# Bounding attention scores by channel maxima, in place of a pass for each row's greatest score

## The chip, the cores and the metric

One core of one Trainium2 chip. The metric is the device time of one execution in microseconds (us). The runs of one kernel on one chip agree within some 0.3%. All runs quoted here are fast: none was more than 1.5% above the fastest of its kernel. In the views of the profile PE is TensorE, PEld its loads of weights, DVE VectorE, ACT ScalarE, POOL GpSimd and SP SyncE; a q after the name means the engine's queue. The granted clock is TensorE's, 1.00 being full speed. PSUM is the memory that TensorE writes its results to.

## The reference

Four residual layers on `x` of shape (2, 128, 64, 64) in float32. Two of them hold softmax attention over all 4096 positions; the other two (depthwise convolutions, and quaternion products of Fourier transforms) are not touched by the change.

```python
# layer 0: four heads of 32 channels; q1 and k1 are divided by their norms over the tokens
attn1 = softmax(einsum('bhnc,bhmc->bhnm', q1, k1) * temperature, axis=-1)
out1  = einsum('bhnm,bhmc->bhnc', attn1, v)
# ... a second, small attention over channels, projections, norms
# layer 3: eight heads of 16 channels
a = softmax(einsum('bhcq,bhck->bhqk', q, k) / sqrt(128), axis=-1)
o = einsum('bhqk,bhck->bhcq', a, v)
```

A softmax subtracts something from each row's scores so that the exponentials don't overflow. Any shift gives the same result in exact arithmetic. The kernel before subtracts each row's greatest score; it has to compute all scores once to find that, and a second time to use them.

## The kernel before

Heads lie in groups of partitions, and a block `qm` holds one head's rows of q, zero elsewhere, so that a matmul over all 128 partitions gives one head's scores. The pass for the greatest scores (comments and some arguments cut):

```python
def _max_pass(...):                                   # line numbers in the profile
    for qt in range(NQT):                             # 32 tiles of 128 queries
        qm = blocks[qt % len(blocks)]
        _own_rows(nc, qm, q, ...)                     # GpSimd copies          L163
        for kc in range(NCH):                         # 8 chunks of 512 keys
            for p in range(0, nh, 2):                 # pairs of heads
                ps = ps_pool.tile([128, 2, CH], F32, tag="sp", name="ps_max")
                for jj in range(2):
                    nc.tensor.matmul(ps[:, jj, :], qm[:, p + jj, :],
                                     k[:, kc * CH : (kc + 1) * CH], ...)     # L175
                nc.vector.tensor_reduce(pm[:, p : p + 2, qt, kc], ps, AX.X, ALU.max)  # L182
                yield
    # [cut] for each head: reduce over chunks, negate, transpose, DMA into row d of q
```

The attention then works on the scores with keys in partitions; row `d` of q, times a row of ones in k, subtracts the maximum:

```python
def _attn_pass(...):
    for qb in range(NCH):                             # 8 blocks of 512 queries
        qm = blocks[qb % len(blocks)]
        _own_rows(nc, qm, q, ..., d + 1, nh)
        for kt in range(NQT):                         # 32 tiles of 128 keys
            for p in range(0, nh, 2):
                ps = ps_pool.tile([128, 2, CH], F32, tag="sp", name="ps_s")
                # [cut] two matmuls k-tile x qm                               # L224
                w = p_pool.tile([128, 2, CH], F32, tag="weights", name="weights")
                nc.scalar.activation(w, ps, AF.Exp)                           # L232
                # [cut] two matmuls values x w of the step before, into ps_acc # L207
                yield
```

`top` is the pass for the maxima and `attend` the attention; `_weave(main, side, n)` issues a step of `side` after every n steps of `main`. In layer 0 that is `_weave(top(0), channels_and_values(), 4)`, the pass with the convolutions, then `_weave(attend(0), top(1), 1)` and `attend(1)` alone, for each of two samples; in layer 3 one `top` alone, three woven stages, one `attend` alone.

Of the kernel before, what the change touches and what calls it, by code (L numbers as in the profile page):

```python
# [17 lines left out]
S = H * W  # L18
CH = 512  # tokens of a chunk: one PSUM bank, eight rows of the image
# [5 lines left out]
FROWS = 4  # rows of frequencies of a weight chunk  # L25
# [4 lines left out]
def _blocks():  # L30
    """Constant matrices, by name, each with up to 128 rows."""
    f8 = np.float64
    k = {}
    k["ident"] = np.eye(128)
    k["group"] = np.kron(np.eye(32), np.full((4, 4), 0.25))
    k["center"] = np.eye(128) - 1.0 / 128
    k["mean"] = np.full((128, 128), 1.0 / 128)
    first = dict(k)

    k = {}  # L40
    # Forward over h: rows (w parity, h), columns (w parity, re/im, fh).
    ang = 2 * np.pi * np.outer(np.arange(H), np.arange(FH)) / H
    k["fwd_h"] = np.kron(np.eye(2), np.concatenate([np.cos(ang), -np.sin(ang)], 1))
    # Columns (r, p, i): the channel (r xor p, i) with the sign that W_p has in output r.
    sign = np.array([[1, -1, -1, -1], [1, 1, 1, -1], [1, -1, 1, 1], [1, 1, -1, 1]], f8)
    perm = np.zeros((128, 4, 4, 32))
    for r in range(4):
        for p in range(4):
            for i in range(32):
                perm[(r ^ p) * 32 + i, r, p, i] = sign[r, p]  # L50
    k["perm"] = perm.reshape(128, 512)
    # Forward over w: rows (re/im, w), columns (-im, re, im; fw); of fh and of its mirror image.
    ang = 2 * np.pi * np.outer(np.arange(W), np.arange(FW)) / W
    c, s = np.cos(ang), np.sin(ang)
    k["fwd_w"] = np.concatenate(
        [np.concatenate([s, c, -s], 1), np.concatenate([-c, s, c], 1)], 0
    )
    k["fwd_w_mirror"] = np.concatenate(
        [np.concatenate([s, c, -s], 1), np.concatenate([c, -s, -c], 1)], 0
    )  # L60
    # Back over w: rows (fw, re/im), columns (re/im, w).
    alpha = np.full((FW, 1), 2.0)
    alpha[0] = alpha[-1] = 1.0
    c, s = alpha * c.T, alpha * s.T
    inv = np.stack([np.concatenate([c, s], 1), np.concatenate([-s, c], 1)], 1).reshape(2 * FW, 2 * W)
    k["inv_w"] = inv
    k["inv_w_mirror"] = inv * np.repeat([1.0, -1.0], W)
    # Back over h: rows (re/im, fh).
    ang = 2 * np.pi * np.outer(np.arange(FH), np.arange(H)) / H
    k["inv_h"] = np.concatenate([np.cos(ang), -np.sin(ang)], 0) / (H * W)  # L70
    second = dict(k)

    k = {}
    sel = np.zeros((2, 128, 64))
    for j in range(4):
        for i in range(16):
            sel[j % 2, 32 * j + i, 16 * j + i] = 1
            sel[1 - j % 2, 32 * j + 16 + i, 16 * j + i] = 1
    k["sel_out"], k["sel_sum"] = sel[0], sel[1]
    third = dict(k)  # L80
    return first, second, third


def _packed(blocks):
    """One array of 128 rows, and where each block lies in it."""
    where, at, parts = {}, 0, []
    for name, a in blocks.items():
        full = np.zeros((128, a.shape[1]), np.float32)
        full[: a.shape[0]] = a
        parts.append(full)  # L90
        where[name] = (a.shape[0], at, at + a.shape[1])
        at += a.shape[1]
    return np.ascontiguousarray(np.concatenate(parts, 1)), where
# [12 lines left out]
def _col(nc, pool, src, name):  # L106
    """A vector of 128, one element in each partition."""
    t = pool.tile([128, 1], F32, tag=name, name=name)
    nc.sync.dma_start(t, src.rearrange("(c o) -> c o", o=1))
    return t  # L110


def _weave(main, side, every):
    """Runs `main` with a step of `side` after every `every` steps, then the rest of `side`."""
    for n, _ in enumerate(main):
        if n % every == every - 1:
            next(side, None)
    for _ in side:
        pass


def _group_stats(nc, pool, psum_tile, x, cst, eps_t):
    """Mean and 1 / sqrt(var + eps) of a sample's groups of four channels, per channel."""
# [27 lines left out]
# The heads of a tile lie hs partitions apart. A head has d rows of q and k; row d is 1 in k and  # L151
# minus the row's greatest score in q, and k is zero in what is left. All rows are contracted, q
# being zero in the other heads' rows of a block that one head uses.
# [42 lines left out]
def _attn_pass(nc, p_pool, ps_pool, acc_pool, blocks, q, k, values, hs, d, nh, done):  # L196
    """values(kt, j): what multiplies the weights of head j in key tile kt, with ones for the
    sums. done(qb, acc) takes the products of a block of queries."""
# [18 lines left out]
    for qb in range(NCH):  # L217
        qm = blocks[qb % len(blocks)]
        _own_rows(nc, qm, q, slice(qb * CH, (qb + 1) * CH), hs, d + 1, nh)
# [23 lines left out]
@with_exitstack  # L243
def _layer0(ctx, tc, X, a, cst, eps5):
# [27 lines left out]
    # 1x1 and depthwise 3x3 as one 3x3 convolution: [ci, tap, co].  # L272
# [18 lines left out]
    max_blocks = _zero_blocks(nc, one, 3, NH, 128, "max_block")  # L291

    def inverse_std(pool, y):
        """1 / sqrt(var over channels + eps), in every channel."""
# [25 lines left out]
    def top(t):  # L320
        return _max_pass(nc, small, spp, ident, max_blocks, qs[t], ks[t], HS, D, NH)
# [9 lines left out]
    for b in range(B):  # L331
        x = X[:, b, :]
        with tc.tile_pool(name="l0_xn", bufs=1) as xp, tc.tile_pool(name="l0_ch", bufs=5) as cp:
# [19 lines left out]
            # q1 and k1; the norms over tokens and the temperature go into q1.  # L353
# [17 lines left out]
            for h in range(4):  # L371
# [5 lines left out]
                )  # L377

            def channels_and_values():
                # k2^T q2, summed over the tokens; then its softmax over k2's channels.  # L380
# [52 lines left out]
                # v, the second attention's output, and v with tokens in partitions.  # L433
# [20 lines left out]
            _weave(top(0), channels_and_values(), 4)  # L454

        with tc.tile_pool(name="l0_p", bufs=3) as pp, tc.tile_pool(name="l0_fin", bufs=5) as cp:
            q_blocks = _zero_blocks(nc, cp, 2, NH, CH, "q_block")

            def attend(t):
                # v and ones of an even head, ones and v of an odd one.  # L460
# [3 lines left out]
                def done(qb, ac):  # L464
# [17 lines left out]
                    nc, pp, spp, accp, q_blocks, qs[t], ks[t], values, HS, D, NH, done  # L482
                )

            _weave(attend(0), top(1), 1)
# [18 lines left out]
@with_exitstack  # L504
def _layer1(ctx, tc, X, a, cst, eps5):
# [20 lines left out]
    # t12 has -t10 and +t7.  # L526
# [6 lines left out]
    for b in range(B):  # L533
# [12 lines left out]
        # Pairs of columns with (w parity, h) in partitions; shifts by two columns are whole tiles.  # L546
# [34 lines left out]
        # [a, shift, b], the shifts in falling order.  # L581
# [22 lines left out]
        # The dilated 5x5 straight onto the residual.  # L604
# [29 lines left out]
@with_exitstack  # L634
def _layer2(ctx, tc, X, a, cst, src, eps5):
# [11 lines left out]
    # Transforms over h for fh to 32, the others being conjugates: [channel, b, fh, re/im, w].  # L647
# [32 lines left out]
    # Back over w, rows of frequencies and their mirror images summed: [channel, b, w, re/im, fh].  # L680
    z = one.tile([128, B, W, 2, FH], F32, name="z")
    names = "wxyz"
    for f0 in range(0, H, FROWS):
# [15 lines left out]
        for pair in range(0, FROWS, 2):  # L699
            # (-im, re, im) of what W_p multiplies in output r: [(p, i), row, fw, r, b, 3].  # L700
# [41 lines left out]
        # [(row, o), (r, b), fw, re/im], then with (fw, re/im) in partitions.  # L742
# [37 lines left out]
    # Back over h, onto the residual.  # L780
# [22 lines left out]
@with_exitstack  # L803
def _layer3(ctx, tc, X, a, cst, src, out, eps5):
# [28 lines left out]
    max_blocks = _zero_blocks(nc, one, 3, NH, 128, "max_block")  # L833
# [40 lines left out]
    def attend(b, t, q, k, vt):  # L874
        rows = slice(64 * t, 64 * t + 64)

        # v and ones of an even head, ones and v of an odd one.
# [4 lines left out]
        def done(qb, ac):  # L882
# [14 lines left out]
            nc, pp, spp, accp, q_blocks, q, k, values, HS, D, NH, done  # L897
        )

    def top(q, k):  # L900
        return _max_pass(nc, two, spp, ident, max_blocks, q, k, HS, D, NH)
# [19 lines left out]
def kernel(ctx, tc, a, out, layers=(0, 1, 2, 3)):  # L921
# [3 lines left out]
    for b in range(B):  # L925
        for i in range(4):
            cols = slice(i * (S // 4), (i + 1) * (S // 4))
            nc.sync.dma_start(X[:, b, cols], a["x"][b, :, cols])
# [3 lines left out]
    if 0 in layers:  # L932
        _layer0(tc, X, a, cst, eps5)
    if 1 in layers:
        _layer1(tc, X, a, cst, eps5)
    if 2 in layers:
        _layer2(tc, X, a, cst, a["consts1"], eps5)
    if 3 in layers:
        _layer3(tc, X, a, cst, a["consts2"], out, eps5)
    else:  # L940
        for b in range(B):
            nc.sync.dma_start(out[b], X[:, b, :])
# [3 lines left out]
def _laid_out(inputs):  # L946
    """The inputs in the orders that the chip reads them in."""
# [16 lines left out]
    # Heads of 16 in slots of 32, four a tile, and a one for the greatest scores behind those of k.  # L964
# [8 lines left out]
    # Pairs of heads with ones between them, for the sums.  # L973
# [26 lines left out]
```

## Time and profile before

| | before |
|---|---|
| median of 4 runs | 16,934.2 us (16,918.7 to 16,954.7) |
| busy: TensorE / VectorE / ScalarE | 97% / 29% / 21% of the span |
| matmuls for maxima / scores / values | 6144 each, two instructions apiece |
| mean granted TensorE clock | 0.971 |

The profile is of one execution, with a span of 16,969.8 us. A group's busy time is the union of its instructions; matmuls overlap at their ends, so the pace is better read from how many steps fit into a long stretch. The prediction below shows the lines.

### The profile page before, as it was taken

The numbers are of one execution on the slowest core, as the hardware profiler recorded it, in microseconds if no ns is written. First come the engines' busy times: TensorE is split into PE (matmuls) and PEld (weight loads), VectorE is DVE, ScalarE is ACT, GpSimd is POOL, SyncE is SP. The second block draws the span as 40 slices with busy tenths as digits, with TensorE's granted clock in tenths as the row PEclk, the third lists the DMA queues.
The fourth block names the chain that finished last, engine by engine and source line by source line (L and its number), as shares of the span: only waits on it lengthen the run. The fifth ranks groups of instructions, "written<-read, shape, count | busy, mean of one in ns | idle before, by whom it ended". The sixth has DMA issues, their size and how long they took to land.

```text
span 16969.8 us, 116126 instructions
## 1 busy us (share of the span) xinstructions
PE 16401.0 (97%) x50778; PEld 6151.0 (36%) x50778; DVE 4966.5 (29%) x4328; ACT 3536.5 (21%) x3820; POOL 468.1 (3%) x1029
## 2 busy tenths in 40 slices
PE   8999998999999788899999999999999999999999
PEld 3433322443332246644333333333333333333222
DVE  4432201352320352267422222322223222221000
ACT  1022232102223201100122222222222222222333
POOL 0000000000000100000000000000000000000000
PEclk9999998999999887889999999999999999999999
DMA  0000000000000015400000000000000000000000
GB/s 19 0 0 0 0 0 0 0 0 0 0 1 0 2 17 83 68 2 0 1 1 1 1 1 1 1 1 1 1 1 1 1 1 1 1 1 1 1 1 1
DMA packets 142859, 90.89 MB, mean 5 GB/s; under 512 B 4752, under 2 KB 137616, under 8 KB 142352
## 3 DMA queue, kind: packets, MB, share of 16 engines
q1 hardware_dynamic: 141056, 80.52, 2.9%
q8 instruction: 399, 6.54, 0.2%
q10 hardware_dynamic: 1296, 2.95, 0.1%
q14 instruction: 108, 0.88, 0.0%
HBM read 78.87 MB, written 4.19 MB: 5 GB/s over the span
## 4 chain that ended last, share of the span: by engine, by line
PE 63%; ACT 1%; issue 1%; DVE 0%; POOL 0%; ACTq 0%; DMA 0%; DVEq 0%; POOLq 0%; SPq 0%
PE ps_max L175 22%; PE ps_s L224 21%; PE ps_acc L207 12%; PE ps_freq L735 2%; PE ps_bank L718 1%; PE ps_bank L707 1%; PE ps_bank L614 1%; PE ps_t L585 1%; ACT yt L715 0%; PE ps_bank L622 0%; PE ps_bank L795 0%; PE ps_bank L764 0%; PE ps_bank L572 0%; PE ps_bank L668 0%; PE ps_sp L887 0%
## 5 line engine op out<-in xcount | busy, mean ns | idle before, releaser
L182 DVE TENSOR_REDUCE max_part<-ps_max 128x2 f32<-128x1024 f32 x3072 | 3765.1, 1226 | 7590.7 <-PE ps_max L175 7589.5
L224 PE MATMUL ps_s<-q_block,k 128*128 128x512 f32 x12288 | 5888.7, 602 | 18.6 <-POOL q_block L163 18.6
L175 PE MATMUL ps_max<-k,max_block 128*128 128x512 f32 x12288 | 5842.6, 610 | 11.2 <-ACT weights L232 5.9
L232 ACT ACTIVATE weights<-ps_s 128x1024 f32<-128x1024 f32 x3072 | 3144.9, 1024 | 10551.5 <-PE ps_s L224 10551.4
L175 PEld LDWEIGHTS ps_max<-k,max_block 128*128 128x128 f32 x12288 | 2164.5, 189 | 3662.1 <-issue 2459.3
L224 PEld LDWEIGHTS ps_s<-q_block,k 128*128 128x128 f32 x12288 | 2253.2, 190 | 3313.2 <-issue 2870.5
L207 PE MATMUL ps_acc<-weights,vt 128*32 128x512 f32 (+1 forms) x12288 | 3258.9, 609 | 1.7 <-ACT weights L232 1.7
L207 PEld LDWEIGHTS ps_acc<-weights,vt 128*32 128x32 f32 (+1 forms) x12288 | 497.5, 116 | 2331.9 <-issue 2310.4
L311 PE MATMUL ps_acc<-xn,wc 128*128 128x512 f32 x1440 | 631.3, 594 | 0.0
L470 DVE RECIPROCAL rec<-rec 64x512 f32<-64x512 f32 x32 | 107.0, 3345 | 1468.2 <-ACT rec L469 1468.2
L163 POOL COPY max_block<-q 16x128 f32<-16x128 f32 (+1 forms) x768 | 233.4, 304 | 9288.2 <-PE ps_max L175 8846.6
L885 DVE COPY u<-ps_acc 128x512 f32<-128x512 f32 x32 | 22.1, 690 | 1482.8 <-PE ps_acc L207 1482.8
L311 PEld LDWEIGHTS ps_acc<-xn,wc 128*128 128x128 f32 x1440 | 272.4, 190 | 342.1 <-issue 342.1
L718 PE MATMUL ps_bank<-consts,yt 128*128 128x99 f32 x1024 | 185.5, 338 | 86.2 <-ACT yt L715 86.2
L735 PEld LDWEIGHTS ps_freq<-e,w_r 128*32 128x32 f32 x4224 | 255.8, 153 | 19.0 <-issue 12.7
L735 PE MATMUL ps_freq<-e,w_r 128*32 128x16 f32 x4224 | 259.9, 212 | 2.2 <-DVE e L725 2.2
L735 PE MATMUL ps_freq<-e,w_i 128*32 128x16 f32 x4224 | 255.4, 212 | 0.0
L735 PEld LDWEIGHTS ps_freq<-e,w_i 128*32 128x32 f32 x4224 | 253.0, 157 | 2.8 <-issue 1.4
L163 POOL COPY q_block<-q 17x512 f32<-17x512 f32 (+1 forms) x192 | 115.8, 609 | 4833.5 <-PE ps_s L224 3802.4
L718 PEld LDWEIGHTS ps_bank<-consts,yt 128*128 128x128 f32 x1024 | 160.6, 239 | 219.1 <-ACT yt L715 218.9
L607 DVE SCALAR_TENSOR_TENSOR X<-g,w,X 128x4096 f32<-128x4096 f32 x50 | 234.7, 4693 | 1.8
L725 DVE COPY e<-ps_bank 128x396 f32<-128x396 f32 x128 | 143.4, 1120 | 307.6 <-PE ps_bank L718 307.6
(176 smaller groups left out, 3012.2 us busy)
## 6 DMA issues: line engine op xcount, KB each, us to landing
w_r<-in_L_conv_kr_w SPq DMA_DIRECT2D x16, 528.0 KB, 12.3
w_r<-in_L_conv_kr_x SPq DMA_DIRECT2D x16, 528.0 KB, 11.8
w_r<-in_L_conv_kr_y SPq DMA_DIRECT2D x16, 528.0 KB, 11.9
w_r<-in_L_conv_kr_z SPq DMA_DIRECT2D x16, 528.0 KB, 11.9
w_i<-in_L_conv_ki_w SPq DMA_DIRECT2D x16, 528.0 KB, 5.4
w_i<-in_L_conv_ki_x SPq DMA_DIRECT2D x16, 528.0 KB, 7.7
w_i<-in_L_conv_ki_y SPq DMA_DIRECT2D x16, 528.0 KB, 10.0
w_i<-in_L_conv_ki_z SPq DMA_DIRECT2D x16, 528.0 KB, 11.9
```

The source lines that it names most:

```text
L163: nc.gpsimd.tensor_copy(block[hs * j : hs * j + rows, j, :], q[hs * j : hs * j + rows, cols])
L175: nc.tensor.matmul(ps[:, jj, :], qm[:, p + jj, :], k[:, kc * CH : (kc + 1) * CH], start=True, stop=True,)
L182: nc.vector.tensor_reduce(pm[:, p : p + 2, qt, kc], ps, AX.X, ALU.max)
L207: nc.tensor.matmul(acc[0][r : r + hs, :], values(kt, p + jj), w[:, jj, :], start=(kt == 0), stop=(kt == NQT - 1),)
L224: nc.tensor.matmul(ps[:, jj, :], k[:, kt * 128 : (kt + 1) * 128], qm[:, p + jj, :], start=True, stop=True,)
L232: nc.scalar.activation(w, ps, AF.Exp)
L311: nc.tensor.matmul(out, wc[:, t, grp * C : (grp + 1) * C], xn[:, c * ROWS + t // 3 : (c + 1) * ROWS + t // 3, t % 3 : t % 3 + W], start=(t ...
L585: nc.tensor.matmul(t3[:, lo // 4, : (hi - lo) * C], xt[:, 3 + u, :], xt[:, u + lo : u + hi, :].rearrange("p k c -> p (k c)"), start=(u == ...
L607: nc.vector.scalar_tensor_tensor(xi, g[:, i : i + H, j : j + W], w8[:, s : s + 1], xi, ALU.mult, ALU.add)
L614: nc.tensor.matmul(pv, t9[:, k, :], t2[:, c * ROWS + k : (c + 1) * ROWS + k, 2 : W + 2], start=(k == 0), stop=False,)
L718: nc.tensor.matmul(pe[:, r * 3 * FW : (r + 1) * 3 * FW], yt[:, r * 128 : (r + 1) * 128], k["fwd_w" if fh == m else "fwd_w_mirror"], start= ...
L735: nc.tensor.matmul(out.rearrange("p (x c) -> p x c", c=2), ws[n][:, :, gq * FW + fw], ef[:, :, 1 - n : 3 - n], start=(n == 0), stop=(n == 1),)
```

## The change

A score is a sum over the head's channels of q times k, so it is at most the sum over channels of max|q| times max|k|, maxima over the tokens. That needs two reductions over 4096 elements and one tiny matmul per tile of heads. If all bounds are at most 60, the exponentials can be taken without a shift. If not, a branch at the end runs the full old program, which is compiled in a second time. The core of the diff (two places are put in words; cut are the zeroing of q in layer 0, and that row `d` of q, which held the maximum, is left out of the scores when there is no pass):

```diff
+LIMIT = 60.0
+class _Bounds:
+    def add(self, q, k, heads, psum_tile, small):
+        m = small.tile([128, 2], F32, tag="bd_m", name="bd_m")
+        for i, t in enumerate((q, k)):
+            nc.vector.tensor_reduce(m[:, i : i + 1], t, AX.X, ALU.max, apply_absolute_value=True)
+        p = small.tile([128, 1], F32, tag="bd_p", name="bd_p")
+        nc.vector.tensor_mul(p, m[:, 0:1], m[:, 1:2])
+        ps = psum_tile()
+        nc.tensor.matmul(ps[:, 0:1], heads, p, start=True, stop=True)
+        nc.vector.tensor_copy(self.all[:, self.at : self.at + 1], ps[:, 0:1])
+        self.at += 1
+    def within(self, psum_tile, small, ident):
+        # compare with LIMIT, minimum over columns, transpose, minimum, to int32
 ...
+            if bounds is not None:
+                for t in range(2):
+                    bounds.add(qs[t], ks[t], same_head, acc, small)
-            _weave(top(0), channels_and_values(), 4)
+            if bounds is None: _weave(top(0), channels_and_values(), 4)
+            else: run channels_and_values() alone
-            _weave(attend(0), top(1), 1)
+            _weave(attend(0), top(1) if bounds is None else iter(()), 1)
 ...  # layer 3: top(q, k) becomes bounds.add(q, k, ...) and an empty iterator
+    bounds = _Bounds(nc, keep, 8)
+    layers(bounds)
+    with tc.tile_pool(name="bd_ps", bufs=1, space=PSUM) as ps:
+        flag = bounds.within(...)
+    within = nc.values_load(flag[0:1, 0:1], min_val=0, max_val=1)
+    with tc.If(within < 1):
+        layers(None)
```

More of the change, by code (lines that the diff above doesn't have):

```diff
@@ L147, in _normalized, with _same_head, __init__ @@
     nc.vector.tensor_scalar(out, x, mean, rstd, ALU.subtract, ALU.mult)
+LIMIT = 60.0
+def _same_head(nc, pool, hs):
+    t = pool.tile([128, 128], F32, name="same_head")
+    nc.gpsimd.memset(t, 0.0)
+    for r in range(0, 128, hs):
+        nc.gpsimd.memset(t[r : r + hs, r : r + hs], 1.0)
+    return t
+class _Bounds:
+    def __init__(self, nc, pool, n):
+        self.nc, self.pool, self.at = nc, pool, 0
+        self.all = pool.tile([128, n], F32, name="bounds")
+    def add(self, q, k, heads, psum_tile, small):
+        nc = self.nc
+        m = small.tile([128, 2], F32, tag="bd_m", name="bd_m")
+        for i, t in enumerate((q, k)):
+            nc.vector.tensor_reduce(
+                m[:, i : i + 1], t, AX.X, ALU.max, apply_absolute_value=True
+            )
+        p = small.tile([128, 1], F32, tag="bd_p", name="bd_p")
[5 more added lines that the diff above has]
+    def within(self, psum_tile, small, ident):
+        nc = self.nc
+        assert self.at == self.all.shape[1]
+        ok = small.tile([128, self.at], F32, name="bd_ok")
+        nc.vector.tensor_scalar(ok, self.all, LIMIT, None, ALU.is_le)
+        low = small.tile([128, 1], F32, name="bd_low")
+        nc.vector.tensor_reduce(low, ok, AX.X, ALU.min)
+        ps = psum_tile()
+        nc.tensor.transpose(ps[0:1, 0:128], low, ident)
+        one = small.tile([1, 1], F32, name="bd_one")
+        nc.vector.tensor_reduce(one, ps[0:1, 0:128], AX.X, ALU.min)
+        flag = small.tile([1, 1], mybir.dt.int32, name="bd_flag")
+        nc.vector.tensor_copy(flag, one)
+        return flag
 def _zero_blocks(nc, pool, n, nh, cols, name):
@@ L193, in _max_pass, with _attn_pass @@
     yield
-def _attn_pass(nc, p_pool, ps_pool, acc_pool, blocks, q, k, values, hs, d, nh, done):
+def _attn_pass(nc, p_pool, ps_pool, acc_pool, blocks, q, k, values, hs, rows, nh, done):
     waiting = []
@@ L218, in _attn_pass @@
         qm = blocks[qb % len(blocks)]
-        _own_rows(nc, qm, q, slice(qb * CH, (qb + 1) * CH), hs, d + 1, nh)
+        _own_rows(nc, qm, q, slice(qb * CH, (qb + 1) * CH), hs, rows, nh)
         for kt in range(NQT):
@@ L243, in _layer0 @@
 @with_exitstack
-def _layer0(ctx, tc, X, a, cst, eps5):
+def _layer0(ctx, tc, X, a, cst, eps5, bounds=None):
     nc = tc.nc
@@ L290, in _layer0 @@
             nc.gpsimd.memset(ks[t][HS * j + D : HS * j + D + 1, :], 1.0)
-    max_blocks = _zero_blocks(nc, one, 3, NH, 128, "max_block")
+    if bounds is None:
+        max_blocks = _zero_blocks(nc, one, 3, NH, 128, "max_block")
+    else:
+        for t in range(2):
+            nc.gpsimd.memset(qs[t], 0.0)
+        same_head = _same_head(nc, one, HS)
     def inverse_std(pool, y):
@@ L377, in _layer0 @@
                 )
+            if bounds is not None:
+                for t in range(2):
+                    bounds.add(qs[t], ks[t], same_head, acc, small)
             def channels_and_values():
@@ L452, in channels_and_values @@
                     yield
-            _weave(top(0), channels_and_values(), 4)
+            if bounds is None:
+                _weave(top(0), channels_and_values(), 4)
+            else:
+                for _ in channels_and_values():
+                    pass
         with tc.tile_pool(name="l0_p", bufs=3) as pp, tc.tile_pool(name="l0_fin", bufs=5) as cp:
             q_blocks = _zero_blocks(nc, cp, 2, NH, CH, "q_block")
+            rows_of_q = D + (bounds is None)
             def attend(t):
@@ L481, in attend @@
                 return _attn_pass(
-                    nc, pp, spp, accp, q_blocks, qs[t], ks[t], values, HS, D, NH, done
+                    nc, pp, spp, accp, q_blocks, qs[t], ks[t], values, HS, rows_of_q, NH, done
                 )
-            _weave(attend(0), top(1), 1)
+            _weave(attend(0), top(1) if bounds is None else iter(()), 1)
             for _ in attend(1):
@@ L803, in _layer3 @@
 @with_exitstack
-def _layer3(ctx, tc, X, a, cst, src, out, eps5):
+def _layer3(ctx, tc, X, a, cst, src, out, eps5, bounds=None):
     nc = tc.nc
@@ L831, in _layer3 @@
     nc.sync.dma_start(bv, a["L3_conv_bv"].to_broadcast([128, 192]))
-    max_blocks = _zero_blocks(nc, one, 3, NH, 128, "max_block")
+    if bounds is None:
+        max_blocks = _zero_blocks(nc, one, 3, NH, 128, "max_block")
+    else:
+        same_head = _same_head(nc, one, HS)
     q_blocks = _zero_blocks(nc, one, 2, NH, CH, "q_block")
@@ L896, in attend @@
         return _attn_pass(
-            nc, pp, spp, accp, q_blocks, q, k, values, HS, D, NH, done
+            nc, pp, spp, accp, q_blocks, q, k, values, HS, D + (bounds is None), NH, done
         )
     def top(q, k):
+        if bounds is not None:
+            bounds.add(q, k, same_head, lambda: sp()[:, 0, :], two)
+            return iter(())
         return _max_pass(nc, two, spp, ident, max_blocks, q, k, HS, D, NH)
@@ L920, with kernel @@
 @with_exitstack
-def kernel(ctx, tc, a, out, layers=(0, 1, 2, 3)):
+def kernel(ctx, tc, a, out):
     nc = tc.nc
@@ L924 @@
     X = keep.tile([128, B, S], F32, name="X")
-    for b in range(B):
-        for i in range(4):
-            cols = slice(i * (S // 4), (i + 1) * (S // 4))
-            nc.sync.dma_start(X[:, b, cols], a["x"][b, :, cols])
     cst = _load_consts(nc, keep, a["consts0"], 0)
@@ L931, with layers @@
     nc.vector.memset(eps5, 1e-5)
-    if 0 in layers:
-        _layer0(tc, X, a, cst, eps5)
-    if 1 in layers:
+    def layers(bounds):
+        for b in range(B):
+            for i in range(4):
+                cols = slice(i * (S // 4), (i + 1) * (S // 4))
+                nc.sync.dma_start(X[:, b, cols], a["x"][b, :, cols])
+        _layer0(tc, X, a, cst, eps5, bounds)
         _layer1(tc, X, a, cst, eps5)
-    if 2 in layers:
         _layer2(tc, X, a, cst, a["consts1"], eps5)
-    if 3 in layers:
-        _layer3(tc, X, a, cst, a["consts2"], out, eps5)
-    else:
-        for b in range(B):
-            nc.sync.dma_start(out[b], X[:, b, :])
+        _layer3(tc, X, a, cst, a["consts2"], out, eps5, bounds)
+    bounds = _Bounds(nc, keep, 8)
+    layers(bounds)
+    with tc.tile_pool(name="bd_ps", bufs=1, space=PSUM) as ps:
+        flag = bounds.within(
+            lambda: ps.tile([128, CH], F32, name="ps_flag"), keep, cst["ident"]
+        )
+    within = nc.values_load(flag[0:1, 0:1], min_val=0, max_val=1)
+    with tc.If(within < 1):
+        layers(None)
 def _laid_out(inputs):
```

## The prediction

> **What bounds the kernel now.** I read the page from its top, the busy time per engine first, then the costliest groups.
>
> ```profile
> PE 16401.0 (97%) x50778; PEld 6151.0 (36%) x50778; DVE 4966.5 (29%) x4328; ACT 3536.5 (21%) x3820; POOL 468.1 (3%) x1029
> ...
> L182 DVE TENSOR_REDUCE max_part<-ps_max 128x2 f32<-128x1024 f32 x3072 | 3765.1, 1226 | 7590.7 <-PE ps_max L175 7589.5
> L224 PE MATMUL ps_s<-q_block,k 128*128 128x512 f32 x12288 | 5888.7, 602 | 18.6 <-POOL q_block L163 18.6
> L175 PE MATMUL ps_max<-k,max_block 128*128 128x512 f32 x12288 | 5842.6, 610 | 11.2 <-ACT weights L232 5.9
> L232 ACT ACTIVATE weights<-ps_s 128x1024 f32<-128x1024 f32 x3072 | 3144.9, 1024 | 10551.5 <-PE ps_s L224 10551.4
> ...
> L207 PE MATMUL ps_acc<-weights,vt 128*32 128x512 f32 (+1 forms) x12288 | 3258.9, 609 | 1.7 <-ACT weights L232 1.7
> ```
>
> TensorE is busy throughout; VectorE and ScalarE sit idle waiting for it, while it waits almost never (11.2 us before the 12288 instructions of the maximum pass). So TensorE is the bound and every instruction it loses counts. There are 12288 instructions for 6144 matmuls: an f32 matmul is two of them. The pass for the greatest scores is 3072 steps of two matmuls (four instructions) and one VectorE maximum of 1226 ns. Busy times of groups overlap at their ends, so 5842.6 us overstates what its removal gives. I therefore took the pace from stretches.
>
> Busy time by stretch (columns: stretch, length, then busy us and instruction count of PE, PEld, DVE, ACT, POOL, and clock, DMA share, GB/s): layer 0 with the pass woven in, layer 0 without, the first pass of layer 3 alone, layer 3 woven, layer 3 without.
>
> ```profile
> 1000.00:2000.00 1000.00, 1000.00 (x2589) 352.43 (x2586) 299.76 (x243) 228.98 (x230) 22.22 (x64) 1.00 0.00 0
> 2200.00:2800.00 600.00, 600.00 (x1643) 179.68 (x1642) 32.48 (x24) 216.95 (x217) 6.12 (x10) 1.00 0.00 0
> ...
> 7400.00:8000.00 600.00, 600.00 (x1400) 265.65 (x1399) 428.71 (x350) 0.00 (x0) 25.39 (x88) 1.00 0.00 0
> 8400.00:10400.00 2000.00, 1992.47 (x5177) 681.54 (x5176) 561.79 (x458) 439.30 (x429) 45.80 (x132) 1.00 0.00 1
> ...
> 15600.00:16800.00 1200.00, 1194.44 (x3290) 338.21 (x3288) 38.06 (x28) 417.27 (x408) 14.62 (x24) 1.00 0.01 1
> ```
>
> ScalarE has one exponential per attention step apart from a few others. The same table for the score matmuls of L224 alone, four instructions a step, counts steps exactly:
>
> ```profile
> 1000.00:2000.00 1000.00, 404.10 (x861) 163.62 (x862) 1.00 0.00 0
> 2200.00:2800.00 600.00, 407.39 (x823) 139.16 (x822) 1.00 0.00 0
> ...
> 8400.00:10400.00 2000.00, 805.89 (x1717) 325.93 (x1716) 1.00 0.00 1
> ...
> 15600.00:16800.00 1200.00, 809.08 (x1632) 276.35 (x1632) 1.00 0.01 1
> ```
>
> - Layer 0: woven, 4.63 us a step (1000 over 216); alone, 2.916 (600 over 205.75).
> - Layer 3: woven, 4.662 (2000 over 429); alone, 2.941 (1200 over 408).
> - Pass alone: 600 us over 350 steps, 1.714 us, or 0.429 us an instruction.
>
> The kernel before thus already holds a sample of every attention stage as it will be afterwards, at granted clock 1.00.
>
> **What the Trainium skill says.**
> 1. "FP8 and Floating Point Precision", TensorE Precision Notes: true FP32 takes four passes through the array. The trace has two instructions a matmul at 0.429 us each, 0.858 us in all, which fits four passes of some 0.21 us.
> 2. "TensorE: Matmul & The Clock Gate", What's actually happening: after about 3.4 us of idle the clock is halved, until about as long a busy time. The trace agrees: after 6.15 us idle, 12 score instructions took 8.15 us in place of about 5.2.
> 3. "VectorE: DVE Perf Modes", The perf-mode tier table: tensor_reduce has only the single rate. The trace agrees: 1226 ns for 1024 elements. Another single-rate operation over 4096 f32 (L607) has a median of 4485 ns; I take 4.4 us for the new reductions.
> 4. "Runtime: NRT & Kernel Launch", Instruction fetch mechanics: code is fetched in sequence, and a taken branch beyond the window waits for a fetch. No branch of this kind is in the trace of before.
>
> **The change part by part.** Does the branch run? I evaluated the reference formulas on the given inputs: the bound, the sum over a head's channels of max|q| times max|k|, is at most 0.12 in layer 0 and 21.6 in layer 3, under the limit of 60. So the second program is skipped. The instruction order of the built kernel shows the weaves gone and everything else in place, with eight tiny bound matmuls in TensorE's queue.
>
> (a) Layer 0, first pass woven with convolutions, twice. From the end of the q and k convolutions (220.3 us) to the first score matmul (879.9) are 659.6 us. In it: 256 pass steps at 1.716 = 439.4; 432 convolution instructions at 0.429 = 185.3; 7.5 of idle; 27.4 left for transposes and small matmuls. After: 185.3 + 27.4, plus new waits. The bound matmuls stand in the queue *before* the next convolutions, so TensorE stops for VectorE's chain: the last evacuation of k (3 us), four reductions at 4.4, and the four scalings of q that the timeline shows:
>
> ```profile
> 224.09 4.72 DVE L375 TENSOR_SCALAR q<-q,s 32x4096 f32<-32x4096 f32 x2
> 228.84 0.32 DVE L374 COPY s<-sc 32x1 f32<-32x1 f32 x2
> 229.20 4.76 DVE L375 TENSOR_SCALAR q<-q,s 32x4096 f32<-32x4096 f32 x2
> ```
>
> That is 3 + 17.6 + 9.5 + 1.5 for small ones, 31.7 us, and 3 for a cold clock. Without max steps as filler, v's eight copies show some 0.9 us each (7), eight transposes 0.4 (3), the channel softmax 4, and the first q block has to be zeroed and filled, 8 with its cold clock. Sum 269.4: saved 390, twice is **780 us**.
>
> (b) Layer 0, first attention with the second pass, twice. 1198.4 us from first score matmul (879.93) to that of the next attention (2078.35), 1197.3 in the other sample. After: 256 x 2.916 = 746.5. Saved **903 us**.
>
> (c) Layer 3, first pass alone: 881.8 us from its first matmul (7311.5) to the values' (8193.3). After: two reductions stand there, 8.8, plus their small ones and a cold clock, 13. Saved **869 us**.
>
> (d) Layer 3, three woven stages of 512 steps: 512 x (4.662 - 2.941) = 881 each, **2643 us**.
>
> (e) Their seams. Each of the three later bounds stalls TensorE 11 us ahead of the attention, 33 in all; gone are the transposes of the maxima, their DMA into q and the cold restart before the last attention, 4 + 8 + 15. **6 us lost.**
>
> (f) The end: a transpose, two small VectorE operations, a register load on each engine, the branch. With skill place 4 in mind, **8 us added**, an estimate that no duration backs.
>
> The rest (both depthwise layers, the Fourier layer, both second attentions of layer 0 and the last of layer 3) stays. VectorE's 3765 us are not counted: they lay beside TensorE. Saved 780 + 903 + 869 + 2643 - 6 - 8 = 5181 us. 16929 - 5181 = **11,748 us**. Check: 3072 steps at 1.717 are 5275, and about 94 of new waits remain to be paid.
>
> **Rivals.**
> - *The branch is taken.* Then the old program runs too: about 28,700 us. Against: bounds a third of the limit. An error in the flag or its integer conversion could still do it.
> - *ScalarE becomes the bound, or the weave was free filler.* If a woven step were limited by the exponential and its latency, removing filler would only leave gaps, and the time would stay near 16,900. Against: the exponential takes 1.024 us in a 2.92 us step, and the stages without filler run at 1.00 of the clock with TensorE busy over 99%.
> - *The clock falls in layer 0.* Without filler the bubbles in the convolution stage, or the long bound stalls, could leave it at half rate. Some 210 us of matmul work stands there in each of two stages, so at the very worst 420 us more, 12,170. Against: the q and k convolutions of before run unfilled at full pace; my bubbles are below 1 us.
> - *Bounds are hidden.* If the stalls cost nothing (convolutions overtaking them), 100 us less: 11,650. Against: the order of TensorE's queue.
>
> **Range and chances.** The large terms (b), (c), (d) are read from samples of the same kernel and should hold to 20 us in all. (a) has some 40 us of uncertainty each way, seams and end 30, and the clock leans upwards. Predicted **11,750 us**, 8 in 10 between **11,650 and 11,890**. Faster by over 2%: **0.98**; within 2%: **0.01**; slower: **0.01**, the taken branch.
>
> **What would show it.** Right: no maximum matmuls or reductions; all attention stages at 2.92 to 2.94 us a step at clock 1.00; TensorE idle about 32 us before the bound matmul of each layer 0 sample and 9 to 11 in layer 3; layers 1 and 2 unchanged at some 1455 us; 12288 score instructions, not 24576. Wrong: a span near 28,700 (branch); a step of over 3 us in a stage where the weave was (a wait took its place); granted clock near 0.5 in the convolution stage; a tail of more than 20 us after the last output DMA.

## The result, and the profile after

Ratios here and below are the mean time of one kernel's fast runs over that of the kernel before in the same rounds, so not quite the ratio of the quoted medians.

| | before | after |
|---|---|---|
| median | 16,934.2 us | 11,735.6 us (11,728.8 to 11,736.6, 4 runs) |
| ratio | 1 | 0.6928 (95%: 0.6919 to 0.6938) |
| matmul instructions | 50,778 | 38,483 |
| VectorE busy | 4966.5 us | 1266.9 us |
| mean granted clock | 0.971 | 0.960 |

Busy time per engine, and the costliest groups, after the change (columns: count, then busy us and mean ns, then idle before and who ended it):

```profile
PE 11087.2 (94%) x38483; PEld 3789.2 (32%) x38483; DVE 1266.9 (11%) x1244; ACT 3534.2 (30%) x3820; POOL 241.2 (2%) x265
...
L278 PE MATMUL ps_s<-q_block,k 128*128 128x512 f32 x12288 | 6100.6, 619 | 5.5 <-POOL q_block L217 5.5
L286 ACT ACTIVATE weights<-ps_s 128x1024 f32<-128x1024 f32 x3072 | 3143.2, 1023 | 5930.5 <-PE ps_s L278 5930.4
...
L261 PE MATMUL ps_acc<-weights,vt 128*32 128x512 f32 (+1 forms) x12288 | 3259.3, 609 | 0.8 <-ACT weights L286 0.8
```

The scores (now L278) and values (L261) are as many as before, the maxima are gone, and TensorE still waits for ScalarE 0.8 us in all. That alone refutes the rival in which the exponential becomes the bound. The scores' busy time rose from 5888.7 to 6100.6 us without more work; probably the overlap at the ends falls differently to the neighbours, which no run here shows; it is why busy times were not used for the sum.

The pace of the stages that had the pass woven in, read from the score matmuls (stretch, length, busy and count of PE and of PEld, clock, DMA share, GB/s): the first attention of layer 0, then two formerly woven stages of layer 3:

```profile
600.00:1200.00 600.00, 407.20 (x821) 139.15 (x822) 1.00 0.00 0
...
5800.00:7000.00 1200.00, 808.55 (x1631) 276.35 (x1632) 1.00 0.00 1
7300.00:8500.00 1200.00, 809.08 (x1632) 276.05 (x1631) 1.00 0.00 1
```

That is 600 / 205.5 = 2.92 us a step in layer 0 and 1200 / 408 = 2.941 in layer 3, at clock 1.00: what the unwoven stages of before had shown.

The new stall in layer 0. First TensorE in the timeline, then VectorE over the same time (start, length, then the instruction, and in brackets the idle time before it and what ended it):

```profile
209.45 14.76 PE L370 MATMUL ps_acc<-xn,wc 128*128 128x512 f32 x34
246.60 0.56 PE L184 MATMUL ps_acc<-bd_p,same_head 128*128 128x1 f32 x2 [22.40 <-DVE bd_p L182]
255.64 0.56 PE L184 MATMUL ps_acc<-bd_p,same_head 128*128 128x1 f32 x2 [8.48 <-DVE bd_p L182]
256.06 6.42 PE L370 MATMUL ps_acc<-xn,wc 128*128 128x512 f32 x11
```

```profile
227.01 4.40 DVE L178 TENSOR_REDUCE bd_m<-k 128x1 f32<-128x4096 f32 x1
...
232.12 4.72 DVE L434 TENSOR_SCALAR q<-q,s 32x4096 f32<-32x4096 f32 x2
...
237.22 4.42 DVE L178 TENSOR_REDUCE bd_m<-q 128x1 f32<-128x4096 f32 x1
241.55 4.71 DVE L434 TENSOR_SCALAR q<-q,s 32x4096 f32<-32x4096 f32 x2
246.29 0.16 DVE L182 TENSOR_TENSOR bd_p<-bd_m 128x1 f32<-128x1 f32 x1
246.37 4.41 DVE L178 TENSOR_REDUCE bd_m<-k 128x1 f32<-128x4096 f32 x1
250.81 0.16 DVE L185 COPY bounds<-ps_acc 128x1 f32<-128x1 f32 x1
250.89 4.41 DVE L178 TENSOR_REDUCE bd_m<-q 128x1 f32<-128x4096 f32 x1
```

The two bound matmuls of a sample, of one column each, hold up all convolutions behind them for 30.9 us (22.40 + 8.48), though these read nothing of theirs: in the trace they follow directly behind the second bound matmul, in the order of TensorE's queue. They do share two PSUM buffers with the bounds. That alone does not explain the wait: the first bound had been copied out of its buffer at 250.97 (L185), and the convolutions still stood until 256.06. Over the whole run, TensorE's waits list 61.8 us of this in layer 0 and 41.8 us in layer 3:

```profile
PE ps_acc L184 <- DVE bd_p L182: 61.8, 4, 22.4
PE ps_sp L184 <- DVE bd_p L182: 41.8, 4, 10.7
```

### The profile page after: what moved, and what is told of

It reads as the page before. It is cut to its first block, busy times and chain, and to the rows that moved or that the text cites. A ratio compares the mean times of both kernels' runs of the same rounds, so it can differ in the third digit from the quotient of the medians.

```text
span 11733.5 us, 86756 instructions
## 1 busy us (share of the span) xinstructions
PE 11087.2 (94%) x38483; PEld 3789.2 (32%) x38483; DVE 1266.9 (11%) x1244; ACT 3534.2 (30%) x3820; POOL 241.2 (2%) x265
## 4 chain that ended last, share of the span: by engine, by line
PE 61%; ACT 1%; DVE 1%; issue 1%; POOL 0%; ACTq 0%; DVEq 0%; POOLq 0%
PE ps_s L278 33%; PE ps_acc L261 17%; PE ps_freq L802 2%; PE ps_bank L785 1%; PE ps_bank L774 1%; PE ps_bank L681 1%; PE ps_t L652 1%; ACT yt L782 1%; PE ps_bank L689 1%; PE ps_bank L862 1%; PE ps_bank L831 0%; PE ps_bank L639 0%; PE ps_bank L735 0%; DVE bd_m L178 0%; PE ps_sp L957 0%
## 5 line engine op out<-in xcount | busy, mean ns | idle before, releaser
L278 PE MATMUL ps_s<-q_block,k 128*128 128x512 f32 x12288 | 6100.6, 619 | 5.5 <-POOL q_block L217 5.5
L278 PEld LDWEIGHTS ps_s<-q_block,k 128*128 128x128 f32 x12288 | 2084.6, 189 | 4022.1 <-issue 2333.1
L261 PE MATMUL ps_acc<-weights,vt 128*32 128x512 f32 (+1 forms) x12288 | 3259.3, 609 | 0.8 <-ACT weights L286 0.8
L261 PEld LDWEIGHTS ps_acc<-weights,vt 128*32 128x32 f32 (+1 forms) x12288 | 497.3, 116 | 2330.9 <-issue 2301.5
L955 DVE COPY u<-ps_acc 128x512 f32<-128x512 f32 x32 | 22.1, 692 | 5799.2 <-PE ps_acc L261 5799.2
L217 POOL COPY q_block<-q 16x512 f32<-16x512 f32 (+1 forms) x192 | 116.5, 607 | 8293.0 <-PE ps_s L278 7676.5
L802 PEld LDWEIGHTS ps_freq<-e,w_r 128*32 128x32 f32 x4224 | 255.8, 153 | 18.1 <-issue 11.4
L782 ACT COPY yt<-ps_bank 128x512 f32<-128x512 f32 x128 | 74.9, 585 | 369.9 <-PE ps_bank L774 369.9
L774 PE MATMUL ps_bank<-consts,y 128*128 128x512 f32 x256 | 177.7, 784 | 0.0
L363 DVE RECIPROCAL r<-sd 128x512 f32<-128x512 f32 x32 | 107.3, 3353 | 166.9 <-ACT sd L361 166.9
L960 DVE RECIPROCAL rec<-ps_sp 64x512 f32<-64x512 f32 x32 | 107.4, 3355 | 64.7 <-PE ps_sp L958 64.7
```

Source lines behind the costliest of these rows:

```text
L261: nc.tensor.matmul(acc[0][r : r + hs, :], values(kt, p + jj), w[:, jj, :], start=(kt == 0), stop=(kt == NQT - 1),)
L278: nc.tensor.matmul(ps[:, jj, :], k[:, kt * 128 : (kt + 1) * 128], qm[:, p + jj, :], start=True, stop=True,)
L774: nc.tensor.matmul(pt, y[:, b, m, :, :].rearrange("p c w -> p (c w)"), k["perm"], start=True, stop=True,)
L782: nc.scalar.copy(yt, pt)
L802: nc.tensor.matmul(out.rearrange("p (x c) -> p x c", c=2), ws[n][:, :, gq * FW + fw], ef[:, :, 1 - n : 3 - n], start=(n == 0), stop=(n == 1),)
```

## The experiments

The prediction was right, so the runs test whether it was right for its reasons. Theory: the gain is the time that TensorE spent streaming the columns of the maximum matmuls; it adds up stage by stage; and the price of the change is the bound matmuls' place in TensorE's queue, plus the branch. Rivals: VectorE's reductions and their waits were the cost; the cost was per instruction or per weave; the guard's price lies in VectorE's time or in the doubled program.

### Only VectorE's reduction taken away

On the kernel before; TensorE does all its work.

```diff
-nc.vector.tensor_reduce(pm[:, p : p + 2, qt, kc], ps, AX.X, ALU.max)
+nc.vector.tensor_reduce(pm[:, p : p + 2, qt, kc], ps[:, :, 0:2], AX.X, ALU.max)
```

> The kernel before, with VectorE's maximum over two scores of each 512 in place of all (any shift leaves a softmax the same, so the result stays right); TensorE's work is unchanged. Theory (VectorE's 3765 us lay beside TensorE): 16,900 to 16,940. Rival (the reduction and its waits are what the pass cost): 3000 us less or more.

Measured: 16,916.9 us, ratio 0.9987 (0.9970 to 1.0003), the result correct. The reductions in this run (minimum, median and maximum in ns):

```profile
L182 DVE TENSOR_REDUCE max_part<-ps_max x3072: 91/164/166, 235.9 to 15385.9; 128x2 f32<-128x4 f32 x192
```

The reduction fell from 1226 to 164 ns (median), over 3072 of them some 3260 us of VectorE's time, and the run stayed the same within its noise. VectorE's share was hidden; the first rival falls.

### A quarter of the columns, as many instructions

```diff
-    nc.tensor.matmul(ps[:, jj, :], qm[:, p + jj, :], k[:, kc * CH : (kc + 1) * CH], ...)
+    nc.tensor.matmul(ps[:, jj, 0:128], qm[:, p + jj, :], k[:, kc * CH : kc * CH + 128], ...)
-nc.vector.tensor_reduce(pm[...], ps, AX.X, ALU.max)
+nc.vector.tensor_reduce(pm[...], ps[:, :, 0:128], AX.X, ALU.max)
```

> The kernel before, with the maximum pass over 128 keys of each 512: as many matmul instructions, a quarter of their columns. Theory (columns through TensorE are the price, 0.429 us for 512, and a weight load of 0.19 us or so bounds the short one): a step falls from 1.716 to between 0.5 and 0.9 us, so 16,934 becomes 13,200 to 14,450. Rival (the price is a fixed one for each instruction or each weave): above 16,000.

Measured: 13,032.9 us, ratio 0.7696 (0.7683 to 0.7709), correct. That is below the range expected. The score matmuls of a woven and the unwoven stage of layer 3 tell the size of a step (columns as above):

```profile
6400.00:7800.00 1400.00, 777.09 (x1651) 281.76 (x1649) 1.00 0.01 1
...
11600.00:12900.00 1300.00, 877.42 (x1771) 299.56 (x1769) 1.00 0.00 1
```

Woven, 1400 / 412.75 = 3.392 us; alone, 1300 / 442.75 = 2.936. The narrow maximum step adds 0.456 us, or 0.114 us an instruction, against 0.429 for the wide: a ratio of 0.27 for a quarter of the columns. With 3072 x (1.717 - 0.456) = 3874 us of the measured 3907, the price is columns. The floor I had put in the expectation was wrong: in the pass that runs alone in layer 3 the narrow matmuls follow each other every 0.112 us (2048 instructions from 5966.4 to 6196.0 us), while their weight loads are still listed at 192 ns each, one overlapping the next. The rival with a fixed price for each instruction or weave falls.

### The change in one layer at a time

```diff
-        _layer0(tc, X, a, cst, eps5, bounds)
+        _layer0(tc, X, a, cst, eps5, None)          # layer 0 keeps its pass
-    bounds = _Bounds(nc, keep, 8)
+    bounds = _Bounds(nc, keep, 4)
```

> The change in layer 3 alone; layer 0 keeps the pass for the greatest scores. Theory (terms a and b of the prediction, 780 and 903, measured some 30 more for a): 11,735 plus 1,690 to 1,725, so 13,425 to 13,460. Rival (the gain comes from a change of state of the whole chip, such as the clock, and does not split by stage): a number that does not add up with the converse run.

The converse run passes `None` to layer 3.

> The change in layer 0 alone; layer 3 keeps the pass. Theory (terms c, d, e: 869 + 2643 - 6): 11,735 plus 3,480 to 3,520, so 15,215 to 15,255; with the converse run the two gains sum to 5,198 within 15 us. Rival: they do not add.

| | median | ratio | gain over before |
|---|---|---|---|
| layer 3 changed alone | 13,444.8 us | 0.7936 (0.7924 to 0.7948) | 3492.6 us |
| layer 0 changed alone | 15,230.2 us | 0.8992 (0.8977 to 0.9007) | 1709.4 us |
| both (the change) | 11,735.6 us | 0.6928 (0.6919 to 0.6938) | 5198.6 us |

Each gain is against the median of before of its own rounds (16,937.4, 16,939.6, 16,934.2). The two add to 5202.0, 3 us from the whole. Both are in their ranges and correct, and nothing is left that a state of the whole chip would have to account for.

### What the guard costs: no guard at all

The changed kernel without `bounds.add`, flag, branch and second program; right for these inputs only.

```diff
-            bounds.add(...)                                  # both layers
-    with tc.tile_pool(name="bd_ps", bufs=1, space=PSUM) as ps:
-        flag = bounds.within(...)
-    within = nc.values_load(flag[0:1, 0:1], min_val=0, max_val=1)
-    with tc.If(within < 1):
-        layers(None)
```

> The changed kernel without bounds, flag, branch and second program (right for these inputs only). Theory: the whole price of the guard is the stalls (104 us), their cold clocks (8 to 12) and the tail (about 10): 11,735 becomes 11,610 to 11,625. Rival (the guard costs next to nothing, the stalls are hidden elsewhere): 11,720 or more.

Measured: 11,627.7 us (11,604.2 to 11,645.5, 5 runs), ratio 0.6864 (0.6855 to 0.6873), correct. The median misses the expected range by 3 us, and the runs spread over 41 us. The profiled one was the fastest. The traces say where such differences come from: the stretch from the first to the last frequency matmul of layer 2, whose code no kernel changed, took 797 us in the profiled run of before, 771 after, 777 in the next run below and 763 here. So the guard's price is better read from the traces outside layer 2.

### What the guard costs: the bound matmuls moved to the end

The products of maxima are kept as columns of one tile, and two matmuls at the end sum them over the heads.

```diff
-        p = small.tile([128, 1], F32, tag="bd_p", name="bd_p")
-        nc.vector.tensor_mul(p, m[:, 0:1], m[:, 1:2])
-        ps = psum_tile()
-        nc.tensor.matmul(ps[:, 0:1], heads, p, start=True, stop=True)
-        nc.vector.tensor_copy(self.all[:, self.at : self.at + 1], ps[:, 0:1])
+        nc.vector.tensor_mul(self.prod[:, self.at : self.at + 1], m[:, 0:1], m[:, 1:2])
 ...  # in within(), ahead of the comparison:
+        n = self.at // 2
+        for i in range(2):
+            ps = psum_tile()
+            nc.tensor.matmul(ps[:, 0:n], _same_head(nc, small, (64, 32)[i]),
+                             self.prod[:, n * i : n * i + n], start=True, stop=True)
+            nc.vector.tensor_copy(self.all[:, n * i : n * i + n], ps[:, 0:n])
```

> The changed kernel with its bound matmuls moved to the end (the products of channel maxima are kept, two matmuls at the end sum them). Theory: the new cost in the middle is TensorE standing in its queue before the bound matmuls, 61.8 us in layer 0 and 41.8 us in layer 3 by the trace, plus some 2 us of cold clock each time. Most of it goes, the first stall of layer 3 may stay in another form: 11,735 becomes 11,630 to 11,645. Rival (the reductions occupy VectorE and whatever waits for it, wherever the matmuls stand): no change, 11,735.

Measured: 11,628.3 us (11,623.2 to 11,635.5, 5 runs), ratio 0.6862 (0.6853 to 0.6872), correct: faster than the change by about 1%, the intervals apart, and 2 us beyond the expected range. The convolutions now run on where the stall was (TensorE's timeline):

```profile
204.73 33.64 PE L374 MATMUL ps_acc<-xn,wc 128*128 128x512 f32 x78
238.21 0.60 PE L460 MATMUL ps_sp<-consts,raw 128*128 128x128 f32 x4
```

The reductions are still there, eight times two at 4.41 us on VectorE, so VectorE's time is not what most of the price was. The price of the guard by stage, each the difference to the kernel without it:

| stage (from, to) | no guard | the change | sums at the end |
|---|---|---|---|
| start to last matmul with `w_po` (projection) in layer 0 | 4073.0 us | +64.0 | +1.5 |
| first q projection to last score matmul of layer 3 | 6103.8 us | +54.2 | +10.1 |
| last sum's copy out of PSUM to the end | 10.78 us | +6.6 | +5.5 |

Together 124.8 us in the change, 17.1 with the sums at the end. The 10.1 us left in layer 3 are VectorE's after all: at its first bound the two reductions (5519.12 to 5527.86 us) stand in VectorE's queue before the operations that take the values out of PSUM (L945), and TensorE waits 7.57 us for these (L939). At the three later bounds the stages are as long as without a guard, to 0.1 us. So the rival holds for some 10 of the 125 us. This version keeps the guard and its second program, beats both kernels, and is the one to use. Its guard's 17.1 us are 0.15% of its time; by the medians alone (11,628.3 and 11,627.7) the two could not be told apart.

### What the guard costs: the branch

```diff
-    within = nc.values_load(flag[0:1, 0:1], min_val=0, max_val=1)
-    with tc.If(within < 1):
-        layers(None)
```

> The changed kernel with bounds and flag computed, but without register load, branch and second program. Theory: the register load (0.5 to 0.8 us) and the branch with its fetch are what stands between the flag at 11,724 and the end of the span at 11,733.5, so 7 to 9 us less, 11,727. Rival (the doubled program or its instruction fetch slows the whole run): more than 30 us less.

Measured: 11,721.0 us (11,716.8 to 11,738.7), ratio 0.6920 (0.6910 to 0.6929): 14.6 us less, where 7 to 9 had been expected; the times alone are inconclusive, as the interval overlaps that of the change. By the traces, of the 14 us between the profiled spans 7 lie in layer 2 (764 against 771 us), the noise named above. The tail, from the last sum's copy (L955) to the end of the span, is 11,716.16 to 11,733.54 = 17.4 us with the branch and 11,708.46 to 11,719.24 = 10.8 without, as in the kernel before (10.8). Load and branch cost 6.6 us, a little less than expected, and the doubled program costs the rest of the run nothing that shows: about 1 us is left between the spans.

### The branch taken

```diff
-LIMIT = 60.0
+LIMIT = 10.0
```

> The changed kernel with a limit of 10 in place of 60, which the bounds of layer 3 (21.6) exceed: the branch goes into the old program. Theory: the two times in sequence, 11,735 + 16,930 less a launch's fixed part, 28,620 to 28,670, with a right result. Rival (a larger price for entering cold code): over 28,750.

Measured: 28,666.2 us (2 runs), ratio 1.6923 (1.6889 to 1.6956), correct: within the expected range, and the sum of the two programs (11,735.6 + 16,934.2 = 28,669.8). So the fallback works, and an input outside the bound pays 69% over the kernel before. The timeline at the branch:

```profile
11714.37 0.14 DVE L201 CAST bd_flag<-bd_one 1x1 int32<-1x1 f32 x1
11715.24 0.85 ACTq L333 DMA_DIRECT2D w_dw<-in_L_conv_w_dw  x2
```

ScalarE's queue issues its first DMA of the second program 0.73 us after the flag is ready: that path falls through. The change's own trace shows the other way, the jump over the second program. There the register load takes 0.46 to 0.79 us by engine, and from the start of its compare-and-branch (L1019) to its next instruction each queue needs 3.5 to 3.8 us; on TensorE's queue the branch itself is listed at 3430 ns. In the run that fell through, the branches at this place are listed at 45 to 87 ns, and the next instruction starts 0.09 to 0.15 us after the branch did. So the jump is over half of the 6.6 us. SyncE's queue then pauses another 2.7 us, from 11,729.5 to 11,732.2, before the last instructions; what that is stays open.

## Why the prediction was right

Predicted 11,750, measured 11,735.6 us, range 11,650 to 11,890. Term by term, from traces at the same events (saved, in us):

| term | predicted | measured |
|---|---|---|
| (a) layer 0, pass woven with convolutions | 780 | 403.8 + 404.2 = 808 |
| (b) layer 0, first attentions | 903 | 450.7 + 450.8 = 901.5 |
| (c) + (d) + (e) layer 3 | 3506 | 3502.8 |
| (f) end | -8 | -6.6 |
| sum | 5181 | 5205.7 |

(a) is from 659.6 to 255.8 us in the first sample (end of the q and k convolutions at 224.0 to the first score at 479.84), and from 856.1 to 452.0 in the second, measured from its first normalization matmul. (b) is from the first score of a sample to its first normalization matmul after both attentions, 1952.0 to 1501.2 and 1950.3 to 1499.6. Layer 3 is from the last k projection ahead of the first pass to the last sum's copy, 9648.4 to 6145.6. The profiled spans differ by 5236, more than the medians' 5199, mostly because layer 2 took 26 us longer in the profiled run of before; that layers 1 and 2 stay unchanged, as forecast, can be checked only to within this noise.

- **TensorE is the bound, and the columns of its matmuls are what the pass cost**: shown, by the run with a quarter of the columns and by that without VectorE's work.
- **The unwoven stages are a sample of what comes**: shown, to 2 us in 900 and 3 in 3500. A slip on the way: the lines give 215.25 and 429.25 woven steps, not 216 and 429, so 4.646 and 4.659 us a step, not 4.63 and 4.662. In (d) that is some 4 us; (b) does not rest on it.
- **The bound matmuls hold up the queue**: shown. The guard's total was put at 123 us (twice 34.7, 13, 33, 8) and is 124.8; moving the matmuls takes 108 of it away. That the total is so close is luck: layer 0 was put at 69.4 and is 64.0, layer 3 at 46 and is 54.2, the end at 8 and is 6.6.
- **The one mis-sized term is (a), 28 us too small.** Its large parts held; the small new waits were overdrawn. Each sample was given 56.7 us of them. Measured in the first: stalls and cold clock 32.5 in place of 34.7; v's eight copies 0.7 each, 5.6 in place of 7; the eight transposes and the softmax 0 in place of 7, because one or more convolutions stand in the queue between a copy and its user; the first q block 2.7 in place of 8, its cold clock falling behind the first score and so into (b). That is 41 in all, 16 less; the matmuls took some 2 more than the 212.7 allowed for them. Net 14, twice. The order of TensorE's queue, which I had, shows those convolutions in between.
- **The clock rival fails**: the granted clock was 1.00 in the stretches above, and in layer 0's convolutions only the first ones after the stall were slow (36 instructions in 17.15 us, later 30 in 13.04, or 0.43 each). The mean fell from 0.971 to 0.960 because stages at full clock got shorter: what was lost to the clock did not grow, 0.029 x 16,970 = 492 us before and 0.040 x 11,734 = 469 after.
- **The branch**: not taken in the change, as the bounds of 21.6 foretold; its cost of 6.6 us against an estimate of 8 that had no duration to stand on, so that this one came out is luck too.

## What to carry to other kernels

Where the bound engine runs a stage both with and without some extra work, the profile of before can already hold the time after; count steps in long stretches there instead of summing busy times. Then ask where the new instructions stand in each engine's queue: eight matmuls of one column whose operand came late cost some 100 us here, and moving them to the end, where nothing waits behind them, took 108 of the guard's 125 us away. The queue of the other engine counts as well: of the 17 us left, 10 come from reductions that stand in VectorE's queue before work for which TensorE waits. A guard with a full fallback costs little when its check is kept out of the bound engine's way, here 0.15%.

## What the Trainium skill lacked or had wrong

- "Runtime: NRT & Kernel Launch", Instruction fetch mechanics, names the fetch stall of a taken branch without a number, and puts a load of registers from HBM at about 200 ns for each; "Advanced Engine Details and Errata", Control Flow Timing, gives about 108 ns for a compare-and-branch. Here load and jump to the end cost 6.6 us, with 3.5 to 3.8 us from each engine's branch to its next instruction (no run tells that this is the fetch); where the branch fell through it took 45 to 87 ns. The load of the flag, which lies in a tile on the chip and not in HBM, took 462 to 789 ns by engine.
- "TensorE: Matmul & The Clock Gate", Measured speedup vs the span model: by its model, column-tiled matmuls overlap almost wholly, though its own table has 2.38 times for three, 79% of that. The pairs of f32 value matmuls here, on different columns of the array, take 2.916 - 1.716 = 1.20 us a pair, where two in sequence would take 1.72 and full overlap 0.86: 1.43 times for two, 72%. The section does not speak of f32, and no run here tells why.
- No page has how far a stage that streams weights by DMA can move between runs of the same code: layer 2, from its first to its last frequency matmul, took from 757 to 797 us over the profiled runs, more than several of the effects studied here.
